# Four-layer graph network on one core: x2 @ w2 computed before layer 2, w3 applied in layer 2, adjacency of layers 2 and 3 from a uint8 copy

## The chip, the cores and the metric

The kernel runs on one core of one Trainium2 chip. The metric is the device time of one launch in microseconds (us). The core's engines are named as in the profile: PE multiplies matrices (PEld is its loading of weights), DVE, ACT and POOL work on rows of SBUF, SP only issues transfers. Each engine works through its own instructions in order and waits on semaphores for the others. A transfer is issued by an engine's queue (SP, ACT or POOL here) and then runs beside the engines.

## The reference, cut to what matters

Input: x of 4096 x 256 floats, adj of 4096 x 4096 floats that are 0 or 1, symmetric, about 32 ones in a row. Every layer is `x = layernorm(x + layer(x))`.

```python
# layer 0
h = concat([x, adj @ x / max(deg, 1)]);  out = relu(h @ W + b)
# layer 1, two steps n = 0, 1;  R = (adj + I) with rows divided by their sums
A  = top_p_attention(Xa)          # per row: softmax of q.k, its largest entries up to a mass of 0.9
Xf = R @ Xf;  Xa = A @ Xa;  Z += Xf @ U1[n].T + Xa @ U2[n].T
out = layernorm(X + Z) * g + b
# layer 2;  edge[i] = sum_j adj[i,j] * adj[j,i]
out = concat([x, adj @ x, edge]) @ weight + bias      # weight: 513 x 256, called w2
# layer 3;  A_norm = (adj + I) scaled by degree^-1/2 on both sides
out = relu((A_norm @ x) @ W + b)                      # W called w3
```

The results of layers 0 to 2 are called x1, x2 and x3 below.

## The kernel before, in words

The 4096 rows are 32 tiles of 128 (`NT`, index `it` of the rows being made, `jt` of the rows being summed over). A product with adj takes for each row tile 32 matmuls of 128x512 into one PSUM bank, one for each `jt`. 512 columns, because the 256 columns of x are held as two halves that add up to x: the upper bits in columns 0 to 255, the rest in 256 to 511. `split` makes them (a DVE mask, an ACT copy, a DVE subtraction), `load_halves` loads a whole matrix in eight chunks of 512 KB through two buffers and splits it into a resident tile `xh`. `transposed` turns a tile of 128x256 with two PE transposes and copies it from PSUM with ACT (buffer `xt`).

*Layer 0* (L215 to L318). POOL loads adj with a cast to uint8 (`a8`, L248), SP stores that copy to `adj8_d` (L249), ACT casts pieces of 128x1024 to the matmul's type (L251), and `adj_matmul` (L168) multiplies. ACT's queue loads x, then w0 and two biases, then w1 and w2t, of which PE makes the query weights `wq_sb` (L227 to L229).

*Layer 1* (two steps, `run_step`). For each row tile it makes the R-product (L652), the row's 4096 logits and exponentials `e`, finds the top-p threshold on DVE, and multiplies by the kept entries: gathered rows (L729), or eight pieces of four transposes of `e` each (L712) with their products (L737). The function `pieces` lays these eight pieces out and lets other work be hung onto them (`ops`, by number of the piece). Rows whose threshold the quick search doesn't reach are put off: their numbers are collected in a list, and one extra tile of such rows in step 0, four in step 1 (`put_off`) are taken up again, from rows gathered by POOL. A put-off tile goes through stages, in which DVE brackets the threshold with probes over the whole row (`bracket`, `settle`); PE sums a flag for it (L554). `advance` runs one stage, `finish` all that are left and then the eight pieces; then come, hung onto the next tile's pieces, `s1` (`mix`: the U products and the residual) and `s2` (two normalizations and the store of x2). Normal tiles are stored by SP, put-off ones scattered by POOL to the rows in their list (`put`, L758) in `x2_d`.

The last two put-off tiles, the third and fourth ("job 2", "job 3"), are finished behind the last normal tile:

```python
for job in jobs:
    last = finish(job, last)
for fs in last:
    for f in fs:
        f()
```

Three row buffers of 16 KB a partition, `es[0..2]`, hold the exponentials in step 1; the two jobs use `es[2]` and `es[0]`.

*Layers 2 and 3* (L1026 on). SP loads x2 back through `load_halves`. POOL loads adj from its float input, 512 KB a piece and four pieces a tile, into the matmul's type (`adj_piece`, L137), four buffers. `l2_end` of a tile stands behind the products of the next tile: it adds the two halves, transposes x2's tile and the sum, multiplies with w2 (four matmuls of 128x256, L1052), adds bias, edge term and residual, normalizes to x3, scales it by dinv (degree^-1/2) and splits it into the halves `yh` for layer 3. `l3_end` scales the summed tile by dinv, adds x3 times dinv squared, transposes, multiplies with w3 (two matmuls, L1075), and ends with relu, residual, normalization and the store.

The order of instructions on each engine is made by a scheduler when the program is built, from the order in which the code issues them and from which buffers are free; the functions below say what is issued, not where it comes to stand.

## Time and profile before

| | us |
|---|---|
| median of 3 runs | 3377.89 (3377.06 to 3378.86) |
| the profiled execution, its own time | 3410.96 |
| its span | 3409.3 |
| PE busy in it | 3032.2 (89%) |
| DVE, ACT, POOL busy | 2382.9 (70%), 1598.1 (47%), 920.8 (27%) |

By stage, from windows on the trace (us of the stage, PE busy, DVE busy, ACT busy, granted PE clock, GB/s moved):

| stage | from, to | length | PE | DVE | ACT | clock | GB/s |
|---|---|---|---|---|---|---|---|
| start | 0, 44 | 44 | 4.4 | 17.2 | 13.2 | 1.00 | 178 |
| layer 0 | 44, 360 | 316 | 316.0 | 270.5 | 170.2 | 1.00 | 136 |
| layer 1, step 0 | 360, 1460 | 1100 | 965.5 | 774.4 | 695.2 | 0.96 | 119 |
| step 1, normal tiles | 1460, 2675 | 1215 | 1106.1 | 1004.6 | 627.5 | 0.96 | 36 |
| last put-off tiles, start of layer 2 | 2675, 2822 | 147 | 64.8 | 95.1 | 25.0 | 0.72 | 80 |
| layer 2 | 2822, 3113 | 291 | 291.0 | 118.3 | 41.1 | 1.00 | 245 |
| layer 3 | 3113, 3409 | 296 | 284.4 | 102.9 | 25.8 | 1.00 | 254 |

The profile is of one execution. Times on its page count from the start of the span. Busy times of engines overlap and don't add up to the span. The stage limits are chosen by eye at the slices in which the picture changes; the layers overlap by a tile or two at them.

### The profile page before, as it was taken

The page shows a single profiled execution, that of the slowest core. Times are in us where ns is not written, and L with a number is a line of the kernel's source. Part 1 is how long each engine was busy: PE and PEld are TensorE (multiplying, and loading weights), DVE is VectorE, ACT ScalarE, POOL GpSimd, SP SyncE. Part 2 cuts the span into 40 slices and gives each one's busy share as a digit, 9 for nine tenths or more (in the row PEclk, how much of TensorE's full clock was granted, in tenths as well). Part 3 has the DMA queues.
Part 4 walks back from the last instruction along what each step waited for, and adds up shares of the span by engine and source line. Part 5 has one row for each costly group of instructions (what it writes and reads, how often), then busy time and mean ns, then how long its engine had stood idle before and what let it go on. Part 6 is the DMA issues. An engine that isn't in the chain of part 4 may idle for free. (4 is left out here: it accounts for less than half of the span.)

```text
span 3409.3 us, 46023 instructions
## 1 busy us (share of the span) xinstructions
PE 3032.2 (89%) x14780; PEld 2486.4 (73%) x14780; DVE 2382.9 (70%) x7082; ACT 1598.1 (47%) x2846; POOL 920.8 (27%) x1170
## 2 busy tenths in 40 slices
PE   5999879999999997789989899989997549999998
PEld 4888667777777775568877677877786437887776
DVE  6888858777777776357988886989799654443333
ACT  4555656666766764455555454645553211111000
POOL 1111246666666664100000001001000112222332
PEclk9999999999999997889999999999999769999999
DMA  8888357777777775141001110011011038888887
GB/s 156 149 141 136 73 98 117 130 135 132 133 131 132 132 133 132 61 131 30 24 22 23 33 38 26 30 32 38 29 38 19 15 103 247 244 247 244 266 270 227
DMA packets 233760, 383.52 MB, mean 112 GB/s; under 512 B 33089, under 2 KB 158849, under 8 KB 233505
## 3 DMA queue, kind: packets, MB, share of 16 engines
q0 software_dynamic: 83328, 238.78, 35.3%
q1 hardware_dynamic: 133200, 125.72, 13.1%
q10 hardware_dynamic: 16976, 15.95, 1.5%
q8 instruction: 120, 1.97, 0.3%
q14 instruction: 136, 1.11, 0.1%
HBM read 423.45 MB, written 57.54 MB: 141 GB/s over the span
## 5 line engine op out<-in xcount | busy, mean ns | idle before, releaser
L652 PE MATMUL acc_r<-xh,adjq 128*128 128x512 f32 x2048 | 615.8, 431 | 31.3 <-ACT adjq L649 21.0
L737 PE MATMUL acc_bank<-xa,at 128*128 128x256 f32 x2304 | 568.2, 388 | 31.0 <-ACT at L715 30.4
L638 POOL DMA_INDIRECT G<-x_d,cols x512 | 498.8, 974 | 331.4 <-PE acc_bank L729 159.7
L737 PEld LDWEIGHTS acc_bank<-xa,at 128*128 128x128 f32 x2304 | 425.5, 194 | 92.7 <-ACT at L715 41.3
L652 PEld LDWEIGHTS acc_r<-xh,adjq 128*128 128x128 f32 x2048 | 379.9, 192 | 131.7 <-ACT adjq L649 46.5
L399 DVE MAX8 cand<-e 128x8 f32<-128x256 f32 x1024 | 381.8, 415 | 130.0 <-ACT e L381 115.8
L649 ACT CAST adjq<-adj 128x512 fp32r<-128x512 uint8 x512 | 316.0, 619 | 312.9 <-issue 94.2
L380 PE MATMUL lg<-kS,q 128*128 128x512 f32 x1104 | 395.6, 444 | 17.8 <-ACT e L381 10.2
L381 ACT COPY e<-lg 128x512 f32<-128x512 f32 x552 | 320.2, 586 | 193.7 <-PE lg L380 171.0
L192 POOL TENSOR_TENSOR rstd<-ve,mhalf 128x1 f32<-128x1 f32 x168 | 103.3, 615 | 899.9 <-DVE ve L190 853.3
L729 PE MATMUL acc_bank<-G,dg 128*128 128x256 f32 x1024 | 275.1, 390 | 33.7 <-DMA G<-x_d,cols 26.7
L496 DVE FIND_INDEX8 cols<-top,e 128x8 uint32<-128x4096 f32 x64 | 282.8, 4419 | 0.0
L168 PE MATMUL acc<-xh,adjt 128*128 128x512 f32 x1024 | 261.5, 407 | 22.7 <-ACT xh L144 18.0
L168 PE MATMUL acc<-yh,adjt 128*128 128x512 f32 x1024 | 257.4, 403 | 3.8 <-DMA adjt<-in_adjt 3.4
L168 PE MATMUL acc<-xh,a 128*128 128x512 f32 x1024 | 258.1, 404 | 1.6 <-ACT a L251 1.6
L729 PEld LDWEIGHTS acc_bank<-G,dg 128*128 128x128 f32 x1024 | 193.9, 193 | 82.7 <-DMA G<-x_d,cols 36.0
L137 POOL DMA_DIRECT2D adjt<-in_adjt x256 | 139.6, 545 | 419.8 <-PE acc L168 316.9
L715 ACT COPY at<-at_ps 128x512 f32<-128x512 f32 x296 | 173.9, 589 | 148.3 <-PE at_ps L712 146.9
L168 PEld LDWEIGHTS acc<-xh,adjt 128*128 128x128 f32 x1024 | 192.3, 191 | 67.9 <-ACT xh L144 19.1
L168 PEld LDWEIGHTS acc<-yh,adjt 128*128 128x128 f32 x1024 | 189.8, 188 | 49.0 <-DMA adjt<-in_adjt 4.1
L168 PEld LDWEIGHTS acc<-xh,a 128*128 128x128 f32 x1024 | 191.4, 189 | 43.9 <-ACT a L251 1.7
L712 PE MATMUL at_ps<-ident,e 128*128 128x128 f32 x1184 | 183.6, 279 | 42.9 <-DVE e L629 29.1
(277 smaller groups left out, 4948.4 us busy)
## 6 DMA issues: line engine op xcount, KB each, us to landing
adjt<-in_adjt POOLq DMA_DIRECT2D x256, 512.0 KB
adj<-adj_d SPq DMA_DIRECT2D x256, 128.0 KB
a<-in_adjt POOLq DMA_DIRECT2D x64, 256.0 KB
adj_d<-a SPq DMA_DIRECT2D x64, 256.0 KB
adjn<-in_adjn POOLq DMA_DIRECT2D x64, 256.0 KB
x_d<-x SPq DMA_DIRECT2D x64, 128.0 KB
G<-x_d,cols POOLq DMA_INDIRECT x512
xf_d<-xf_new SPq DMA_DIRECT2D x64, 128.0 KB
```

Source lines behind the costliest of these rows:

```text
L168: nc.tensor.matmul(acc, a[:, j, :], halves(jt), start=(jt == 0), stop=(jt == NT - 1))
L380: nc.tensor.matmul(pl[:, :LC], q[k], kS[:, s], start=(k == 0), stop=(k == 1))
L381: nc.scalar.copy(l[:, s], pl[:, :LC])
L399: nc.vector.max(dst[:, 8 * g : 8 * g + 8], src[:, g * GW : (g + 1) * GW])
L496: nc.vector.max_index(st["at"][:, 8 * r : 8 * r + 8], t8, st["e"][:, :N])
L638: nc.gpsimd.indirect_dma_start(out=g, out_offset=None, in_=x1_d, in_offset=bass.IndirectOffsetOnAxis(ap=st["at"][:, k : k + 1], axis=0))
L649: nc.scalar.copy(a, cur["a8"][:, g % 2 * GP : (g % 2 + 1) * GP, :])
L652: nc.tensor.matmul(acc_r, a[:, j, :], xf[:, jt, :], start=(jt == 0), stop=False)
L712: nc.tensor.transpose(ps[:, j, :], e[:, (g * G + j) * P : (g * G + j + 1) * P], ident)
L715: nc.scalar.copy(at[:, :G, :], ps[:, :G, :])
L729: nc.tensor.matmul(acc_a, dg[:, k % 4, :], st["G"][k], start=(k == 0), stop=(k == KEPT - 1))
L737: nc.tensor.matmul(acc_a, ats[g][:, j, :], cur["xa"][:, jt, :], start=(jt == 0), stop=(jt == NT - 1))
```

## The change

Four things are changed.

1. Query weights: `w1` and `w2t` are loaded on ACT's queue ahead of x, and no longer behind it and w0.
2. x2 @ w2 before layer 2. A new DRAM matrix `zu_d` of 512 columns takes for each row of x2 its product with the neighbour part of w2 (columns 0 to 255, "z") and with the own part (256 to 511, "u"). `z_room` loads the weights into the row buffer that the two jobs do not use, with four buffers for tiles of x2 and four for results; `zu` transposes a tile, makes two matmuls of 128x512 and copies the result from PSUM with ACT; `zu_tile` loads a tile of x2 and stores the result. The first 16 tiles are hung onto job 2's pieces, the other 16 are issued between job 3's stages, four at each. Rows that were put off are done once more from `h` in `s2` and scattered to `zu_d`. So that every row of `x2_d` that is read has been written, layer 0 stores its x1 of the last tile there too.
3. w3 in layer 2. Layer 2 aggregates z, so that the sum over neighbours needs no w2 product; `l2_end` adds u, loaded from `zu_d`. The new `l2_y`, two tiles later, transposes x3, multiplies with w3, scales by dinv and splits into `yh`; so `l3_end` has no product, and adds the tile's own two halves of `yh` in place of x3 times dinv squared.
4. Adjacency in layers 2 and 3 comes from `adj8_d`, in pieces of 128 KB of uint8 issued by SP (five buffers), cast by ACT to the matmul's type (four buffers).

The diff, cut to the lines that these four points touch:

```diff
...
+    zu_d = dram.tile([N + P, 2 * D], F32, name="zu_d")
...
-    def load_halves(scratch, src, queue):
+    def load_halves(scratch, src, queue, cols=slice(None)):
...
-                queue.dma_start(t, all_rows(src)[:, s, :])
+                queue.dma_start(t, all_rows(src)[:, s, cols])
...
+        w1_sb = l0.tile([DA, D], F32, name="w1_sb")
+        nc.scalar.dma_start(w1_sb, w1)
+        w2t_sb = l0.tile([DA, DA], F32, name="w2t_sb")
+        nc.scalar.dma_start(w2t_sb, w2t)
         x0h = load_halves(l0.tile([P, 4 * J0 * D], F32, name="scratch"), x, nc.scalar)
         w0_sb = load_w(l0, w0, "w0_sb")
         lb_sb = load_bcast(l0, ln_b, "lb_sb")
         b0_sb = load_bcast(l0, b0, "b0_sb")
-        w1_sb = l0.tile([DA, D], F32, name="w1_sb")
-        nc.scalar.dma_start(w1_sb, w1)
-        w2t_sb = l0.tile([DA, DA], F32, name="w2t_sb")
-        nc.scalar.dma_start(w2t_sb, w2t)
...
+            if it == NT - 1:
+                nc.sync.dma_start(rows(x2_d, it), x1[:, it, :])
...
                 ln_apply(h, h, ln_stats(h))
                 put(x2_d, st, h)
+                if "z" in cur and st["tile"] is None:
+                    put(zu_d, st, zu(h))
             return [s1] if n + 1 < STEPS else [s1, s2]
+        def z_room(e):
+            w = e[:, : 4 * D].rearrange("p (c o) -> p c o", c=2)
+            for k in range(2):
+                nc.sync.dma_start(w[:, :, k * D : (k + 1) * D],
+                                  w2[(1 - k) * D : (2 - k) * D, :].rearrange("(c p) o -> p c o", p=P))
+            cur["z"] = {"w": w, "x": e[:, 4 * D : 8 * D].rearrange("p (k o) -> p k o", o=D),
+                        "out": e[:, 8 * D : 16 * D].rearrange("p (k o) -> p k o", o=2 * D), "n": 0}
+        def zu(x):
+            z = cur["z"]
+            xt = transposed(x)
+            ps = ps_acc.tile([P, 512], F32, tag=("acc", "nef")[z["n"] % 2], name="zu_ps", bufs=1)
+            for c in range(2):
+                nc.tensor.matmul(ps, xt[:, c, :], z["w"][:, c, :], start=(c == 0), stop=(c == 1))
+            out = z["out"][:, z["n"] % 4, :]
+            z["n"] += 1
+            nc.scalar.copy(out, ps)
+            return out
+        def zu_tile(i):
+            x = cur["z"]["x"][:, i % 4, :]
+            nc.sync.dma_start(x, rows(x2_d, i))
+            nc.sync.dma_start(rows(zu_d, i), zu(x))
...
-            def finish(job, last):
+            def finish(job, last, todo=(), beside=()):
                 while not advance(job):
-                    pass
+                    for f in todo[:4]:
+                        f()
+                    todo = todo[4:]
+                for f in todo:
+                    f()
                 ops = {}
+                for k, f in enumerate(beside):
+                    ops.setdefault(k * NLC // len(beside), []).append(f)
                 for k, fs in enumerate(last):
-                    ops[k + 1] = fs
+                    ops.setdefault(k + 1, []).extend(fs)
...
-            for job in jobs:
-                last = finish(job, last)
+            todo = []
+            if n > 0:
+                z_room(es[1 - NT % 2])
+                todo = [lambda i=i: zu_tile(i) for i in range(NT)]
+            for k, job in enumerate(jobs):
+                if k + 1 < len(jobs):
+                    last = finish(job, last, beside=todo[: NT // 2])
+                    todo = todo[NT // 2 :]
+                else:
+                    last = finish(job, last, todo)
             for fs in last:
                 for f in fs:
                     f()
@@ -1024,20 +1073,27 @@
     with tc.tile_pool(name="l23", bufs=1, reuse_waits="tile") as l23:
-        w2_sb = load_w(l23, w2[: 2 * D, :], "w2_sb")
+        zh = load_halves(l23.tile([P, 4 * J0 * D], F32, name="scratch"), zu_d[:N, :], nc.sync, slice(0, D))
         w2e_sb = load_bcast(l23, w2[2 * D, :], "w2e_sb")
         b2_sb = load_bcast(l23, b2, "b2_sb")
         w3_sb = load_w(l23, w3, "w3_sb")
         b3_sb = load_bcast(l23, b3, "b3_sb")
-        x2h = load_halves(l23.tile([P, 4 * J0 * D], F32, name="scratch"), x2_d[:N, :], nc.sync)
         yh = [pool.tile([P, NT // 2, 2 * D], F32R, tag="X", name=f"yh{k}") for k, pool in enumerate((xpool, l23))]
-        dinv2 = l23.tile([P, NT], F32, name="dinv2")
-        nc.vector.tensor_mul(dinv2, dinv, dinv)
+        def y_halves(jt):
+            return yh[2 * jt // NT][:, jt % (NT // 2), :]
         def main(it, halves):
             acc = ps_acc.tile([P, 512], F32, tag=("acc", "nef")[it % 2], name="acc")
-            adj_matmul(l23, acc, it, halves, lambda it, c: adj_piece(l23, adjt, it, c, "adjt"))
+            for c in range(NJP):
+                a8 = l23.tile([P, JP, P], U8, tag="a8", name="a8", bufs=5)
+                nc.sync.dma_start(a8, adj8_d[it][:, c * JP : (c + 1) * JP, :])
+                a = l23.tile([P, JP, P], F32R, tag="adjt", name="a", bufs=4)
+                nc.scalar.copy(a, a8)
+                for j in range(JP):
+                    jt = c * JP + j
+                    nc.tensor.matmul(acc, a[:, j, :], halves(jt), start=(jt == 0), stop=(jt == NT - 1))
             return acc
         def l2_end(it, acc):
@@ -1046,48 +1102,59 @@
             nc.vector.tensor_add(nn, nn, acc[:, D:])
             xi = l23.tile([P, D], F32, tag="res", name="x2i", bufs=2)
             nc.sync.dma_start(xi, rows(x2_d, it))
-            xt = transposed(xi, nn)
-            ps = half("mm")
-            for c in range(4):
-                nc.tensor.matmul(ps, xt[:, c, :], w2_sb[:, c, :], start=(c == 0), stop=(c == 3))
+            u = l23.tile([P, D], F32, tag="u", name="u", bufs=2)
+            nc.sync.dma_start(u, rows(zu_d, it)[:, D:])
             nc.vector.tensor_add(xi, xi, b2_sb)
+            nc.vector.tensor_add(u, u, xi)
             t = l23.tile([P, D], F32, tag="t", name="t", bufs=2)
-            nc.vector.scalar_tensor_tensor(t, w2e_sb, nef[:, it : it + 1], ps, op0=ALU.mult, op1=ALU.add)
-            nc.vector.tensor_add(t, t, xi)
-            x3 = l23.tile([P, D], F32, tag="h", name="x3", bufs=2)
+            nc.vector.scalar_tensor_tensor(t, w2e_sb, nef[:, it : it + 1], nn, op0=ALU.mult, op1=ALU.add)
+            nc.vector.tensor_add(t, t, u)
+            x3 = l23.tile([P, D], F32, tag="h", name="x3", bufs=3)
             ln_apply(x3, t, ln_stats(t))
             nc.sync.dma_start(rows(x3_d, it), x3)
+            return x3
+        def l2_y(it, x3):
+            xt = transposed(x3)
+            ps = half("mm")
+            for c in range(2):
+                nc.tensor.matmul(ps, xt[:, c, :], w3_sb[:, c, :], start=(c == 0), stop=(c == 1))
             y = l23.tile([P, 1, D], F32, tag="y", name="y", bufs=2)
-            nc.vector.tensor_scalar(y[:, 0, :], x3, dinv[:, it : it + 1], None, op0=ALU.mult)
+            nc.scalar.activation(y[:, 0, :], ps, AF.Copy, scale=dinv[:, it : it + 1])
             up = l23.tile([P, 1, D], I32, tag="up", name="up", bufs=2)
-            split(up, yh[2 * it // NT][:, it % (NT // 2), None, :], y)
+            split(up, y_halves(it)[:, None, :], y)
         def l3_end(it, acc):
             x3 = l23.tile([P, D], F32, tag="res", name="x3i", bufs=2)
             nc.sync.dma_start(x3, rows(x3_d, it))
             a = l23.tile([P, D], F32, tag="agg", name="agg", bufs=2)
-            nc.scalar.activation(a, acc[:, :D], AF.Copy, scale=dinv[:, it : it + 1])
-            nc.vector.scalar_tensor_tensor(a, acc[:, D:], dinv[:, it : it + 1], a, op0=ALU.mult, op1=ALU.add)
-            nc.vector.scalar_tensor_tensor(a, x3, dinv2[:, it : it + 1], a, op0=ALU.mult, op1=ALU.add)
-            xt = transposed(a)
-            ps = half("mm")
-            for c in range(2):
-                nc.tensor.matmul(ps, xt[:, c, :], w3_sb[:, c, :], start=(c == 0), stop=(c == 1))
-            t = l23.tile([P, D], F32, tag="t", name="t", bufs=2)
-            nc.vector.tensor_add(t, ps, b3_sb)
-            nc.vector.scalar_tensor_tensor(t, t, 0.0, x3, op0=ALU.max, op1=ALU.add)
-            o = l23.tile([P, D], F32, tag="h", name="o", bufs=2)
-            ln_apply(o, t, ln_stats(t))
+            d = dinv[:, it : it + 1]
+            nc.scalar.activation(a, acc[:, :D], AF.Copy, scale=d)
+            own = y_halves(it).bitcast(F32)
+            for part in (own[:, :D], own[:, D:], acc[:, D:]):
+                nc.vector.scalar_tensor_tensor(a, part, d, a, op0=ALU.mult, op1=ALU.add)
+            nc.vector.tensor_add(a, a, b3_sb)
+            nc.vector.scalar_tensor_tensor(a, a, 0.0, x3, op0=ALU.max, op1=ALU.add)
+            o = l23.tile([P, D], F32, tag="h", name="o", bufs=3)
+            ln_apply(o, a, ln_stats(a))
             nc.sync.dma_start(rows(out, it), o)
-        for halves, end in ((lambda jt: x2h[:, jt, :], l2_end), (lambda jt: yh[2 * jt // NT][:, jt % (NT // 2), :], l3_end)):
-            acc = None
-            for it in range(NT):
-                new = main(it, halves)
-                if acc is not None:
-                    end(it - 1, acc)
-                acc = new
-            end(NT - 1, acc)
+        done = []
+        for it in range(NT):
+            acc = main(it, lambda jt: zh[:, jt, :])
+            if it > 1:
+                l2_y(it - 2, done.pop(0))
+            if it > 0:
+                done.append(l2_end(it - 1, last))
+            last = acc
+        l2_y(NT - 2, done.pop(0))
+        l2_y(NT - 1, l2_end(NT - 1, last))
+        for it in range(NT):
+            acc = main(it, y_halves)
+            if it > 0:
+                l3_end(it - 1, last)
+            last = acc
+        l3_end(NT - 1, last)
```

## The prediction

> **What bounds the kernel now.** I read the forty slices first, to find the stages; then the chain of waits; then the timeline where the chain is not the same group over and over; then groups by line in one stage.
>
> ```profile
> PE   5999879999999997789989899989997549999998
> DVE  6888858777777776357988886989799654443333
> ACT  4555656666766764455555454645553211111000
> PEclk9999999999999997889999999999999769999999
> DMA  8888357777777775141001110011011038888887
> ```
>
> PE is at nine tenths in all stages but three: the first slice, the middle (1400 to 1535 us) and the slices around 2640 to 2820 us. The last seven slices are layers 2 and 3: PE full, ACT nearly idle, DMA at eight tenths. Windows on them, clean of their ends:
>
> ```profile
> 2825.00:3113.00 288.00, 288.00 (x1311) 233.55 (x1310) 117.43 (x328) 40.21 (x89) 81.48 (x149) 1.00 0.81 245
> 3134.00:3399.00 265.00, 262.21 (x1141) 206.81 (x1139) 89.87 (x240) 22.35 (x62) 80.68 (x147) 1.00 0.87 264
> ```
>
> So both layers are set by what PE must do, the adjacency DMA hiding behind it (PE waited 3.6 us for it in both together). The chain gives the price of each piece: one tile of layer 2, then one of layer 3.
>
> ```profile
> 2835.10 6.50 PE acc L168 x28
> 2842.04 0.92 PE acc L168 x4
> 2842.96 1.81 PE mm_bank L1052 x8
> ...
> 3170.74 6.75 PE acc L168 x29
> 3177.71 0.86 PE acc L168 x3
> 3178.57 0.88 PE mm_bank L1075 x4
> ```
>
> A layer 2 tile starts every 9.67 us (2835.10, 2844.77), a layer 3 tile every 8.71 (3170.74, 3179.45). 32 acc matmuls take 7.44, the four w2 products 1.80, the two w3 products 0.88, two transposes about 0.22. The tail of layer 1 is another matter: there DVE finds the threshold of the last put-off tile and PE waits.
>
> ```profile
> 2697.74 1.02 POOL L758 DMA_INDIRECT x_d<-h,to_last  x1 [0.74 <-DVE lo_l L468]
> 2734.99 0.19 PE L554 MATMUL mm_bank<-ones_col,bad_l 128*1 128x1 f32 x2 [38.31 <-DVE bad_l L530]
> 2753.75 1.94 PE L712 MATMUL at_ps<-ident,e 128*128 128x128 f32 x8 [18.57 <-DVE e L629]
> 2784.40 1.03 POOL L758 DMA_INDIRECT x_d<-h,to_l  x1 [0.31 <-issue]
> 2789.31 0.93 SPq L158 DMA_DIRECT2D scratch<-x_d  x2
> ```
>
> PE stands idle 38.3 us before the flag matmul and 18.6 us after it: 57 us, the room that the change wants to fill.
>
> **The change part by part.** All sums are against the profiled execution (span 3409.3, its own time 3410.96); the median of the runs is 3377.89, 1% less, so a saving counts 0.99 of itself there.
>
> *Query weights.* PE's first matmul (L227) stands ahead of all others and waits for w2t_sb; ACT's copies of it stand ahead of the first adjacency cast:
>
> ```profile
> 33.28 0.69 PE L227 MATMUL mm_bank<-w2t_sb,w_sb 64*128 64x64 f32 x2 [33.28 <-DMA w2t_sb<-in_w2t]
> 39.92 1.04 ACT L251 CAST a<-a 128x1024 fp32r<-128x1024 uint8 x1
> 41.02 10.31 PE L168 MATMUL acc<-xh,a 128*128 128x512 f32 x37 [1.56 <-ACT a L251]
> ```
>
> In the built program of the change the first cast still stands behind the seventh cast of x, which ends at 38.49 in the trace, but the four wq_sb copies (L229) are out of its way: it can start near 38.9 instead of 39.92. x itself is issued two DMA issues later (0.5 us each). Between a loss of 1.0 and a gain of 1.4 I take a gain of **1.0 us**; layer 0 is PE-bound after it and hands it on. Up to the end of layer 1 the built order is otherwise the same, but for one store of tile 31 to x2_d on SP.
>
> *x2 @ w2 in the tail: the work.* Each of 32 tiles adds, on PE, two transposes (0.22) and two 128x512 fp32 products. No such product exists before; eight 128x256 instructions take 1.73 us on L737 (2769.99, 2772.15 less the transposes), so these are 4 instructions of 0.43, 1.71 us. Together 1.93 a tile, 62 us: more than the 57 us of idle time, even if all of it could be used. ACT adds a copy of 128x256 (0.37, as L180) and one of 128x512 from PSUM (0.59, as L381). SP adds a load of 128 KB and a store of 256 KB.
>
> *Where it stands.* PE runs in order, and the built order puts tiles 0 to 13 among the pieces of the third put-off tile (job 2), then the flag matmul of the last one (job 3), then tiles 14 to 31, and only then job 3's transposes (L712). Followed from 2675, where job 2's pieces begin:
> - Tiles 0 to 5 run between the pieces; job 2's remaining work reaches 2701.8.
> - The load of tile 6 waits on SP for the scatter of tile 31 into x2_d, because that scatter may write any row. The scatter is issued one DVE probe later than now (h is normalized behind the third probe): at 2703.5, not 2697.74. A scatter takes 1.03 to issue and 3.9 more until the next reader starts (2784.40 to 2789.31), and a load about 2: tile 6 at 2710.7. PE is idle for 9 us and starts at half clock (L712 at 2753.75: 1.94 for eight transposes; 1.03 warm), 2 us more.
> - Tiles 6 to 13 with the pieces left take 6.6 us a pair (3.42 products, 0.43 each for transposes, pieces' transposes and one product, 1.3 for three more, 0.6 waiting for ACT's copy): the flag matmul is at about 2737.5 instead of 2734.99. DVE's settling needs it but has slack.
> - Tiles 14 and 15 end at 2741. The other eight pairs have nothing beside them: 3.42 of products, and 1.26 from a pair's end to the next product, since ACT must first copy the old result (0.59), then the transposes (0.37). 4.68 a pair, 37.4 us. PE reaches job 3's transposes near **2778.5; now 2753.75**.
> - Its pieces take 24.6 us to the last product (now 21.9: 1.9 for job 2's rows and 2.4 waiting for their h added, 1.7 saved by a warm PE). So +27 there, and mix and both normalizations as now.
> - Behind h comes the new end: transposes, copy, product (half clock after some 5 us of idleness: 3.4), copy, POOL's scatter behind that of x2_d, landing. From h to the first load of zu it is 10.4 us, against 5.3 from h (2784.0) to 2789.31.
>
> Layer 2's first load thus starts at 2821.5 instead of 2789.31: **+32.2 us**.
>
> *Layer 2's start.* Eight chunks of 512 KB with two buffers. Now it takes 33.2 us to the 64th product (2822.5), beside 512 KB adjacency pieces. After, the pieces are 128 KB, so a round of two chunks is 1.9 of splitting and 4.3 of loading (4.1 at 2789.31 to 2793.42, 4.5 in the first stage). Four rounds and the last nine products: 28.8. **-4.4**.
>
> *Steady layers 2 and 3.* From the 64th product to the last one it is 575.9 us now (2822.5 to 3398.35). Layer 2 loses four w2 products and two transposes but gains two w3 products: exactly a layer 3 tile of now, 8.71. ACT's xt copy now stands behind a cast (1.05) that frees up only when the tile before is through: 0.15 more. 30 tiles: 265.8; the last two tiles' w3 work 2.5; a wait of about 1 for the last x3 at the border. Layer 3 is left with 32 products, 7.48 a tile with the overhead of the rows: 239.4. Sum 508.7: **-67.2**.
>
> The new feed has to carry that. ACT casts four pieces a tile. Layer 0 has the same cast from the same shape:
>
> ```profile
> L168 PE MATMUL acc<-xh,a 128*128 128x512 f32 x783 | 196.9, 403 | 0.0
> L251 ACT CAST a<-a 128x1024 fp32r<-128x1024 uint8 x99 | 103.8, 1049 | 106.0 <-PE acc L168 105.2 <-DMA adj_d<-a 0.8
> ```
>
> PE waits 0.0 us there. Per tile ACT would have 4.2 of casts and 1.6 of other work of 8.86 in layer 2, and 4.7 of 7.48 in layer 3; DVE 3.5 (three at 0.48, two at 0.43, normalization 1.2). POOL loses all adjacency issues; SP takes them (0.32 each, 1.3 us a tile, ahead of and behind its loads and stores: a store waits for DVE, and the casts behind it are up to nine pieces, 17 us, ahead).
>
> *A rule that speaks against it.* In the trace four times as many bytes went through: 245 GB/s in layer 2 with pieces of 512 KB, PE waiting 3.6 us. The Trainium skill ("DMA: Bandwidth & Descriptors", section "Anatomy of one DMA — SWDGE (gpsimd) path") gives a transfer of that path 2.0 us plus its bytes over 436 GB/s: 2.3 us for 128 KB, while PE uses a piece up in 1.86. One at a time, a tile would cost 9.2 us in both layers, 62 of them 570 us, and the 67 would shrink to 6: the change would come out 19 us slower. No run here shows that cost for this piece at this rate; with five buffers five are in flight, so I take the rows. For what stands alone the rule is kinder than the trace: 512 KB would land in 3.2 us (trace 4.1) and the scatter in 2.6 (3.9), some 5 us less at layer 2's start. I keep the trace's.
>
> *The end.* Behind the last product there is no transpose, w3 product or copy: ACT 0.47, three DVE 0.48, two 0.43, normalization 2.3, store 3.5. 8.9 against 10.9: **-2.0**.
>
> Sum: -1.0 + 32.2 - 4.4 - 67.2 - 2.0 = **-42.4**, profiled 3368.5; on the median 0.99 of it, 3377.89 - 42.0 = **3336 us**. Bounds: if the tail hid everything, +6 instead of +32; if none of the 62 us, with its copies 75, were hidden, about +80, which would make it slower.
>
> **The rivals.**
> 1. The tail hides better (scatter and copies sooner, PE warm throughout): +6 to +12. For it: 57 us of idle time. Against: 18 tiles stand behind the flag in the order. 3377.9 - 67 = 3311.
> 2. The feed limits a little: layer 3 stays at 8.1 or layer 2 at 9.3, because ACT's in-order queue holds a cast behind a copy that waits for PE. For it: xt, agg and y stand between the casts. Against: layer 0's 0.0. 20 us less gain: 3356.
> 3. Slower: the transfers of the tail. Each pair loads 256 KB and stores 512 KB; at 4.68 us that is 160 GB/s, beside 247 in layer 2, but in one SP queue in which stores waiting for ACT stand ahead of loads, with four buffers. If a pair takes 7.3 us instead of 4.68 over all 16 pairs, the 42 us are gone; at 9, it is +27: 3405. Against: loads stand four tiles ahead in the built order.
> 4. Nothing to see: tail and steady layers cancel (tail +75), near 3378.
>
> **How the numbers follow.** My sum 0.63, rival 1 0.12, rival 2 0.14, rival 3 0.07, rival 4 0.04. The first three are faster: 0.89; same 0.04; slower 0.07 (0.2%, 7 us, being about what a measurement of this kernel can tell from no change). The range takes in rivals 1 and 2 and the 6 us either way of the pair time: 3306 to 3361; my sum's own range is 3322 to 3350.
>
> **What would show it.** In the changed profile: PE full but for one gap near 2702 to 2711; job 3's L712 transposes some 25 us later; layer 2's chain repeating every 8.7 to 8.9 us without L1052, layer 3's every 7.5 without transposes; DMA share in both far under 0.8 and ACT near 0.6. I am wrong in the tail if layer 2's first load comes before 2805 or after 2835; in the layers if PE waits for casts or a tile takes over 9.2 or 8.0.

## The result, and the profile after

The changed kernel took **3316.99 us** (median of 4 runs, 3311.76 to 3319.24) against 3377.47 of the kernel before; ratio 0.982, 95% interval 0.9803 to 0.9837. Two later comparisons of the same pair, each on another chip, gave 0.9848 (0.9827 to 0.987) and 0.9841 (0.9823 to 0.986). In microseconds the gain was 60 in the first comparison, 48 and 51 in these two. Forecast were 3336 and a range of 3306 to 3361, a gain of 42: faster, as said, and by more than said.

The page of the changed kernel's profile (span 3317.5), its forty slices:

```profile
PE   4999878999999997789989898989999786999998
DVE  5888858878777776357988897888799673444444
ACT  4555566777777774455545454555455333666664
PEclk9999989999999998889999999999999898999999
DMA  8888367777777776241000211011011133333332
```

The three slices of PE's row between 2570 and 2820 us read 7, 8 and 6, where the kernel before had 7, 5 and 4 just ahead of its layer 2: the new products stand there. The layers behind it now show ACT at six tenths, and DMA at three instead of eight. Windows on both layers, clean of their ends (from, to, length, then busy time and instructions of PE, PEld, DVE, ACT and POOL, granted clock, DMA share, GB/s):

```profile
2825.00:3075.00 250.00, 249.62 (x1114) 200.41 (x1114) 107.89 (x321) 162.33 (x238) 16.56 (x30) 1.00 0.35 107
3085.00:3300.00 215.00, 215.00 (x951) 178.01 (x950) 102.73 (x265) 134.27 (x148) 15.88 (x29) 1.00 0.35 106
```

PE is still full in both, the clock is still 1.00, and the traffic is 107 GB/s instead of 245 and 264. The chain of waits gives a tile of layer 2, and the last of layer 3:

```profile
2828.61 0.22 PE tr L180 x2
2828.83 1.39 PE acc L1096 x6
2830.21 0.98 PE mm_bank L1121 x4
2831.19 5.95 PE acc L1096 x26
2837.14 0.22 PE tr L180 x2
...
3289.95 13.84 PE acc L1096 x61
```

From transposes to transposes layer 2 takes 8.53 us (2828.61, 2837.14); layer 3 is one unbroken row of products (61 in 13.84, 0.227 each), and by its normalizations a tile comes every 7.25 us.

PE in the tail, from the timeline (start, length, instruction, idle time before it and who ended it):

```profile
2670.51 1.21 PE L180 MATMUL tr<-ident,e 128*128 128x128 f32 x4 [7.07 <-DMA e<-x_d]
2696.94 0.19 PE L559 MATMUL mm_bank<-ones_col,bad_l 128*1 128x1 f32 x2 [0.45 <-DVE bad_l L535]
2701.71 3.70 PE L844 MATMUL zu_ps<-e,xt 128*128 128x512 f32 x8 [0.51 <-ACT xt L182]
2706.36 3.70 PE L844 MATMUL zu_ps<-e,xt 128*128 128x512 f32 x8 [0.51 <-ACT xt L182]
...
2737.81 1.04 PE L717 MATMUL at_ps<-ident,e 128*128 128x128 f32 x8
```

Two tiles of x2 @ w2 take 4.65 us behind the flag matmul (2701.71, 2706.36). Job 3's transposes (L717) follow with no wait shown. They need only the first quarter of `e` to begin (in a run below they start 0.16 us after it), and DVE had that ready at 2715.66:

```profile
2714.38 1.28 DVE L634 SCALAR_TENSOR_TENSOR e<-e,t_thr_l 128x1024 f32<-128x1024 f32 x1
```

PE comes to them at 2737.81, 22 us later.

### The profile page after: what moved, and what is told of

It reads as the page before. It is cut to its first block, busy times and chain, and to the rows that moved or that the text cites. A ratio compares the mean times of both kernels' runs of the same rounds, so it can differ in the third digit from the quotient of the medians.

```text
span 3317.5 us, 46380 instructions
## 1 busy us (share of the span) xinstructions
PE 3005.6 (91%) x14600; PEld 2455.0 (74%) x14600; DVE 2392.3 (72%) x7113; ACT 1883.1 (57%) x3170; POOL 782.1 (24%) x916
## 5 line engine op out<-in xcount | busy, mean ns | idle before, releaser
L643 POOL DMA_INDIRECT G<-x_d,cols x512 | 499.4, 975 | 300.7 <-PE acc_bank L734 161.9
L1093 ACT CAST a<-a 128x1024 fp32r<-128x1024 uint8 x256 | 268.0, 1048 | 147.5 <-PE acc L1096 119.3
L1096 PE MATMUL acc<-xh,a 128*128 128x512 f32 x1024 | 254.9, 402 | 16.9 <-ACT a L1093 13.2
L170 PE MATMUL acc<-xh,a 128*128 128x512 f32 x1024 | 257.9, 404 | 13.3 <-ACT a L253 13.3
L1096 PEld LDWEIGHTS acc<-xh,a 128*128 128x128 f32 x1024 | 190.5, 189 | 60.3 <-ACT a L1093 15.2
L1096 PE MATMUL acc<-yh,a 128*128 128x512 f32 x1024 | 233.7, 390 | 0.0
L170 PEld LDWEIGHTS acc<-xh,a 128*128 128x128 f32 x1024 | 191.7, 190 | 55.1 <-ACT a L253 13.5
L1096 PEld LDWEIGHTS acc<-yh,a 128*128 128x128 f32 x1024 | 192.1, 188 | 39.8
L253 ACT CAST a<-a 128x1024 fp32r<-128x1024 uint8 x128 | 133.9, 1048 | 129.6 <-PE acc L170 117.4
```

The lines of the kernel that those rows point to most:

```text
L170: nc.tensor.matmul(acc, a[:, j, :], halves(jt), start=(jt == 0), stop=(jt == NT - 1))
L643: nc.gpsimd.indirect_dma_start(out=g, out_offset=None, in_=x1_d, in_offset=bass.IndirectOffsetOnAxis(ap=st["at"][:, k : k + 1], axis=0))
L1093: nc.scalar.copy(a, a8)
L1096: nc.tensor.matmul(acc, a[:, j, :], halves(jt), start=(jt == 0), stop=(jt == NT - 1))
```

## The experiments

**A second profile of the kernel before.** The two profiles differ by 92 us in span, the runs by 60. By the stores of `h` (one a tile), the median tile of step 0 took 28.4 us before and 27.3 after, with the same order of instructions.

> The kernel before, unchanged, for a second profile. In the two profiles so far a tile of step 0 takes 28.3 us before and 27.3 after, 37 us over the stage, though the order of instructions there is the same. Theory: this belongs to the one profiled execution of before (3410.96, its runs 3374 to 3379); here step 0 takes 27.3 to 27.5 us a tile and the span is 3377 +- 4. Rival: the change makes step 0 itself faster (one DRAM matrix more, other addresses); then step 0 stays at 28.3 a tile and the span near 3410.

Measured: span 3368.6, ratio to before 0.9997 (0.9984 to 1.0009), a tile of step 0 every 27.3 us. The slow step 0 belonged to that one execution. From here on this profile is the one to compare with; the two agree in the tail and the layers: 9.68 us a tile in layer 2, 8.71 (median) in layer 3, and the border between tail and layers, the first load of layer 2, stands here in this kernel, and below it in the changed one:

```profile
2749.88 0.94 SPq L158 DMA_DIRECT2D scratch<-x_d  x2
```

```profile
2783.55 0.92 SPq L160 DMA_DIRECT2D scratch<-zu_d  x2
```

**The uint8 adjacency alone.**

```diff
-            adj_matmul(l23, acc, it, halves, lambda it, c: adj_piece(l23, adjt, it, c, "adjt"))
+            for c in range(NJP):
+                a8 = l23.tile([P, JP, P], U8, tag="a8", name="a8", bufs=4)
+                nc.sync.dma_start(a8, adj8_d[it][:, c * JP : (c + 1) * JP, :])
+                a = l23.tile([P, JP, P], F32R, tag="adjt", name="a", bufs=4)
+                nc.scalar.copy(a, a8)
...
```

> The kernel before with one part of the change: adjacency of layers 2 and 3 from the uint8 copy (four buffers of uint8 instead of five, for room). Theory: with less than half of the DMA traffic the products follow each other at 0.228 us, as after, instead of 0.2325 (L3: 7.26 for 32 products), so 0.12 to 0.18 a tile over 62 tiles, 7 to 11 us, and 4.4 at layer 2's start: 11 to 15 us faster, ratio 0.9955 to 0.9967. Rival A: the shorter pitch comes from the layers' having fewer other products between, not from the traffic: 4 us, ratio 0.999. Rival B: ACT, which casts four pieces a tile, holds layer 2 up: not faster.

Measured: ratio 0.9983 (0.9974 to 0.9992), 6 us, nearly what rival A gave. Layer 2 takes 9.72 us a tile, layer 3 8.62, at 82 and 90 GB/s. One tile of its layer 3 in the chain of waits, and below it the row of products in the second profile of the kernel before:

```profile
3200.47 6.03 PE acc L1047 x26
3206.50 0.22 PE tr L178 x2
3206.72 1.40 PE acc L1047 x6
3208.12 0.96 PE mm_bank L1082 x4
```

```profile
3210.56 6.74 PE acc L168 x29
```

The 26 products take 6.03, 0.232 each, the same as before at three times the traffic (29 in 6.74). My theory fell: the traffic is not what stretched the products. Rival A put the shorter pitch of the changed kernel down to there being fewer other products between; the run with w3 put back (below) tests that, and it is not the whole of it.

**The other way round: everything but the uint8 adjacency.** The same edit undone in the changed kernel.

> The changed kernel with adjacency of layers 2 and 3 loaded by POOL as floats, 512 KB a piece, as before. A layer 3 tile then moves 2.1 MB of adjacency and 0.26 MB of x3 and output; the most that a slice of before shows is 270 GB/s. Theory: DMA becomes the bound, 8.7 us a tile in layer 3 (now 7.26) and 9.3 in layer 2 (now 8.53), so 46 and 25 us, and 4 at layer 2's start: near 3385 us, not faster than before; the work taken from PE would be worth nothing without the small adjacency. Rival: 270 GB/s was only what PE asked for; then PE stays the bound, 7.44 and 8.7 a tile: 3317 + 15 = 3332.

Measured: 3429.67 us, ratio 1.0162 (1.0142 to 1.0183): slower than the kernel before, and worse than forecast. What PE waited for in both layers (total, times, longest):

```profile
PE acc L170 <- DMA adjt<-in_adjt: 78.7, 61, 3.1
```

Layer 3 moves 277 GB/s and takes 8.42 us a tile, so 270 was indeed near the most that it gets here. Layer 2 takes 11.1 us at only 223 GB/s, by a ring that I had not seen. From its chain of waits:

```profile
2862.53 0.41 DVE x L199
...
2862.96 0.32 SPq L1107
...
2863.37 6.57 DMA x2i<-x_d
...
2872.85 0.67 POOL rstd L194
```

The load of x2 for the next tile stands on SP behind the store of x3, which waits for DVE, and then takes 6.4 to 6.7 us to land beside 512 KB pieces (2.1 to 3.4 in the changed kernel, beside pieces of 128 KB). DVE waits for it, POOL's part of the normalization (`rstd`) waits for DVE, and the next adjacency loads stand behind that on POOL's queue; the normalized tile is then stored, and the ring begins again. In the changed kernel it does not show: there the chain of layer 2 is PE alone. So the parts are not additive: uint8 alone is worth 6 us, the rest alone costs 56, both together gain 48 to 60.

**Half of the tail's new products left out.** Tiles 16 to 31 are not made, so this kernel leaves part of the computation out.

```diff
+            if it >= NT // 2:
+                nc.sync.dma_start(rows(zu_d, it)[:, :D], x1[:, it, :])
+                nc.sync.dma_start(rows(zu_d, it)[:, D:], x1[:, it, :])
...
-                    last = finish(job, last, todo)
+                    last = finish(job, last)
```

> The changed kernel without the x2 @ w2 products of tiles 16 to 31, those issued between the stages of the last put-off tile (their rows of zu_d hold x1, stored in layer 0). Theory: behind the flag matmul they stand 37 us on PE, of which DVE's settling hides all but 18 (DVE has e ready at 2719.3, PE comes to the transposes at 2737.8 in the changed profile); PE then comes cold, 2 us more: layer 2's first load 16 to 18 us earlier, 3300. Rival A: PE is not what the tail's end waits for, nothing changes: 3317. Rival B: the transfers of these tiles hold more up than PE's time: over 25 us, under 3292.

Measured: 3303.71, span 3298.3; the first load of layer 2 comes 172.2 us after SP's last pair of stores to `x2_d` begins (2591.30 to 2763.49), against 193.9 in the changed kernel. 21.7 of the tail's cost go with these 16 tiles, and PE now waits for DVE's first pass over `e`:

```profile
2716.83 1.94 PE L720 MATMUL at_ps<-ident,e 128*128 128x128 f32 x8 [14.96 <-DVE e L637]
```

```profile
2715.39 1.28 DVE L637 SCALAR_TENSOR_TENSOR e<-e,t_thr_l 128x1024 f32<-128x1024 f32 x1
```

The theory gave 16 to 18, because it took DVE's last pass (2719.3) for what the transposes wait for; by the first pass PE was 22 us late, and that is what came back. In the times it is less: the ratio to before is 0.9797 (0.9779 to 0.9816) where the changed kernel has 0.982 to 0.985, some 8 to 17 us.

**The changed kernel again, with the query weights and w3 put back, each by itself.**

> The changed kernel, unchanged, beside the next three on one chip: ratio 0.982 as before. In its profile as in the first: first load of layer 2 some 194 us behind the last store of a normal tile to x2_d, layer 2 at 8.53 and layer 3 at 7.25 us a tile, 13.7 us from the last product to the end. Rival: those were that one execution's own; then they move by some us here.

Measured: 193.2 us to the first load, 8.51 and 7.25 a tile, 13.7 at the end. The readings hold.

```diff
         b0_sb = load_bcast(l0, b0, "b0_sb")
+        w1_sb = l0.tile([DA, D], F32, name="w1_sb")
+        nc.scalar.dma_start(w1_sb, w1)
...
```

> The changed kernel with w1 and w2t loaded behind x and w0 again. In the profiles the store of step 0's first tile starts at 491.1 to 493.4 with the weights behind x and at 495.9 to 496.5 with them ahead. Theory: the two loads ahead of x cost 2 us until the first product (43.02 against 41.02) and some 2 more in layer 0: this store comes back to 491 to 493, 3 to 5 us faster than the changed kernel, ratio to it 0.9987. Rival, the prediction's own step: being ahead gains 1 us; then 1 us slower.

Measured: the first store of `h` comes at 493.6 instead of 497.5, span 3318.8 against 3322.0. In the times it is lost: ratio to before 0.9845 against 0.9848, each with an interval of 0.0043. The profile says a loss of 3 to 4 us from loading the weights first, which the runs can neither show nor refute.

```diff
-            nc.scalar.activation(y[:, 0, :], ps, AF.Copy, scale=dinv[:, it : it + 1])
+            nc.vector.tensor_scalar(y[:, 0, :], x3, dinv[:, it : it + 1], None, op0=ALU.mult)
...
+            xt = transposed(a)
+            ps = half("mm")
+            for c in range(2):
+                nc.tensor.matmul(ps, xt[:, c, :], w3_sb[:, c, :], start=(c == 0), stop=(c == 1))
```

> The changed kernel with w3 applied in layer 3 again (y = dinv * x3 is split in layer 2; transposes, product and bias in layer 3). Theory: PE has the same products to do; layer 2 runs at 7.25 to 7.35 us a tile and layer 3 at 8.5 to 8.6, the sum 15.8 as now, and the end is 1 to 2 us longer: the changed kernel + 1 to 3 us. So the whole saving in the layers comes from w2. Rival A: layer 2 cannot go under 8 us, because each tile also loads u and x2 and stores x3 on SP's queue between the adjacency pieces: + 20 us. Rival B: two products that break up the row of adjacency products cost more where both layers' ends are, + 10.

Measured: 3325.6 against 3320.74, ratio to before 0.9863 (0.9844 to 0.9882) beside 0.9848: not told apart by the times. Layer 2 takes 7.55, layer 3 8.50 a tile, 16.05 together against 15.76. Moving w3 is worth 0.3 us a tile at most, 9 us; the rest of the layers' 83 comes from moving w2 out of them, together with the uint8 adjacency without which it does not pay. Layer 2, now without transposes and products, is the fast one, and layer 3 with them the slow one. That layer 2 stays 0.3 above 7.25 has a place: its first ten tiles or so run at 7.25, and from then on one product a tile, the first of a piece, starts up to 0.7 us late. ACT's copy of `yh` waits there for DVE's split, with two casts behind it in ACT's queue:

```profile
2995.79 0.41 ACT L146 CAST yh<-up 128x256 fp32r<-128x256 f32 x1 [2.94 <-DVE up L145]
```

Layer 3 of this run also answers the question left by the uint8 run, since it has the same breaks in its rows of adjacency products (two transposes, w3 products) as that run's layer 3:

```profile
3200.68 5.91 PE acc L1096 x26
3206.60 0.22 PE tr L180 x2
3206.82 1.39 PE acc L1096 x6
3208.21 0.97 PE mm_bank L1135 x4
```

Here the 26 products take 5.91, 0.227 each; there they took 0.232. The 32 products of a tile take 7.30 here, 7.43 there and 7.25 unbroken. So the breaks account for about 0.05 a tile, and neither they nor the traffic for the other 0.13. What makes the products slower in the kernel before and in its uint8 version stays open.

**Where the new products stand: three tries.** First the room for them goes into the tile of the R-product's matrix, which is free from tile 30 on, and 12 tiles are hung onto tile 30's pieces.

```diff
+                if n > 0 and i == NT - 2:
+                    z_room(hpool.tile([P, 16 * D], F32, tag="H", name="zroom"))
+                    later_zu = [lambda i=i: zu_tile(i) for i in range(NT)]
+                    for k, f in enumerate(later_zu[:12]):
+                        at(k * NLC // 12, f)
...
-                    last = finish(job, last, beside=todo[: NT // 2])
+                    last = finish(job, last, beside=todo[:14])
```

> The changed kernel with the room for x2 @ w2 in the tile that held the matrix of the R-product (free once the last R-product is made), so that 12 of the 32 tiles go beside the pieces of normal tile 30, 14 beside job 2's pieces, and 6 between job 3's stages. Theory: PE is idle for 24 us from tile 30's pieces to tile 31's, where the 12 fit; behind the flag matmul only some 5 tiles are left, which DVE's settling hides; layer 2's first load comes 15 to 20 us earlier: near 3300, ratio to before 0.977. Rival A: the 12 tiles hold tile 30's and 31's own chain up by what they take on PE (23 us): nothing gained, 3317. Rival B: their copies on ACT and their loads on SP's queue delay the settling too: slower than the changed kernel.

Measured: 3318.3 against 3320.74, not told apart by the times, where 3300 was forecast. In the profiled execution the first load of layer 2 comes 10.7 us earlier than in the changed kernel beside it (2777.51 against 2788.22). Job 3's transposes now wait for DVE, but job 2's start 8 us later (2625.76 against 2617.61). They come 8.11 us after PE's last work ahead of them, here and in the two kernels below alike (13.65 of idle time in the changed kernel); the loop over left-over rows (L903) stands between, and the 12 tiles ahead of it pushed it back. That entering the loop costs these 8 us is argued from the place of the gap and not shown. Rival A, for the most part.

Then other places, and beside them the changed kernel once more:

> The changed kernel, unchanged, on the same chip as the next three, so that they can be compared with it: ratio to before 0.982 to 0.985. No theory differs on it.

Measured: 3315.73, ratio 0.9841.

```diff
+        def zu_load(i):
+            nc.sync.dma_start(cur["z"]["x"][:, i % 16, :], rows(x2_d, i))
...
+                for i in range(6, 22):
+                    zu_load(i)
             for k, job in enumerate(jobs):
...
-                    last = finish(job, last, beside=todo[: NT // 2])
+                    last = finish(job, last, beside=todo[:20])
```

> The changed kernel with the room for x2 @ w2 in the tile of the R-product's matrix, which is free from tile 30 on: 6 tiles beside normal tile 30's pieces (the twelve of the last experiment took 13 us too long there), 20 beside job 2's pieces, 6 between job 3's stages; 16 buffers for tiles of x2 instead of 4, and tiles 6 to 21 loaded ahead of the scatter of tile 31, on which the seventh load waits now for 7 us. Theory: the bound of the tail is then DVE's settling of the last put-off tile, no longer PE's row of products: the transposes of job 3 come right after DVE's e, layer 2's first load 16 to 20 us earlier than in the changed kernel; 3301 to 3305, ratio to it 0.9945. Rival A: the flag matmul, now behind 20 tiles, holds the settling up: 8 us less gain. Rival B: the six tiles beside tile 30 delay tile 31 by what they take, 12 us: then only some 6 us are left.

Measured: 3305.16 against 3315.73, ratio to before 0.9811 (0.979 to 0.9831); the span is 3303.6 against 3321.1, the first load of layer 2 at 2767.68 against 2785.47, 17.8 earlier. The load's wait of 7 us is gone, and DVE ends both of PE's waits in the tail:

```profile
2703.03 0.19 PE L559 MATMUL mm_bank<-ones_col,bad_l 128*1 128x1 f32 x2 [2.77 <-DVE bad_l L535]
2721.85 1.06 PE L717 MATMUL at_ps<-ident,e 128*128 128x128 f32 x8 [1.05 <-DVE e L634]
```

The bound has gone over from PE to DVE's settling, and the load came as early as the theory said. The times gained less than the spans, 10.6 us (ratio 0.9968 to the changed kernel, forecast 0.9945); the profiled execution of the changed kernel was the slowest of its four. What is left of the tail's cost, about 14 us (32.0 less 17.8), stands outside this stretch: some 10 of it behind the start of job 3's transposes, from where the first load is 45.8 us off here, 44.3 to 45.7 in the three profiles of the changed kernel, and 35.6 in the kernel before.

```diff
-        zh = load_halves(l23.tile([P, 4 * J0 * D], F32, name="scratch"), zu_d[:N, :], nc.sync, slice(0, D))
+        zh = load_halves(l23.tile([P, 4 * J0 * D], F32, name="scratch"), zu_d[:N, :], nc.sync, slice(0, D), 2)
```

> As the one before, with the query weights behind x again (2 to 4 us) and layer 2's matrix loaded in 16 chunks of 256 KB through four buffers instead of 8 of 512 KB through two. Theory: splitting and loading then overlap better, 64 products are through 25 us after the first load instead of 28.6: 6 to 8 us below the one before. Rival: half of the bytes a transfer cost what the overlap gains; then 2 to 4 us below, from the weights alone.

Measured: **3302.27 us**, ratio to before 0.9799 (0.9777 to 0.982), span 3299.1, 4.5 below the one before, where 6 to 8 were forecast: the first 96 products of layer 2 end 35.5 us after the first load instead of 39.1, as the theory had it for 64, and the first store of `h` comes at 494.9 instead of 497.9. Of these 3 us only 0.6 are left at the first load of layer 2 (2767.05 against 2767.68). It is the lowest time of all kernels with the whole computation, 13 us under the changed kernel's 3315.73 on the same chip; against the one before, the times alone do not separate it.

**The end.**

```diff
-                nc.sync.dma_start(a8, adj8_d[it][:, c * JP : (c + 1) * JP, :])
+                nc.gpsimd.dma_start(a8, adj8_d[it][:, c * JP : (c + 1) * JP, :])
```

> The changed kernel with the uint8 pieces of layers 2 and 3 issued by POOL instead of SP. In all kernels with the uint8 adjacency the last store is followed by 8.6 us until the span's end, in those with float adjacency by 3.5; SP's last wait is for PE's sequencer, 6 us against 0.7 to 1.0. Theory A: it hangs on the pieces being issued by SP; then 3.5 here. Theory B: it hangs on PE's taking its weights from ACT's casts (its waits on semaphores); then 8.6 here too. Layer 2 and 3 per tile as before, 8.53 and 7.25, by both.

Measured, one run: 3313.56, layers 8.5 and 7.25. SP's last waits, in the changed kernel and then here:

```profile
SPq L1195 <- PEq L1195: 6.6, 2, 6.0
SPq L1195 <- DMA out<-o: 1.0, 1, 1.0
```

```profile
SPq L1195 <- PEq L1195: 1.5, 2, 1.0
SPq L1195 <- DMA out<-o: 1.0, 1, 1.0
```

From the last output of DVE to the end it is 3.6 us instead of 8.7. Theory A: the wait for PE's sequencer hangs on who issues the pieces. The other runs agree: 5.7 us with uint8 alone, issued by SP, and 1.0 with float pieces issued by POOL. Why PE's sequencer comes 5 us later when SP issues them stays open.

## Why the prediction was right, point by point

The clean pair of profiles (spans 3368.6 and 3317.5, from separate comparisons) can be cut at the prediction's own joints. The first is the start of the last pair of stores that SP makes to `x2_d`, at 2587.95 and 2589.66; the 64th product of layer 2 is at 2783.07 and at 2812.3 (the 16th of the 48 from 2808.52 to 2819.91); the last product ends at 3357.96 and 3303.79.

| step | predicted | measured |
|---|---|---|
| start, up to that store | -1.0 | +1.7 |
| tail, to the first load of layer 2 | +32.2 | +32.0 (161.9 to 193.9) |
| layer 2's start, 64 products | -4.4 | -4.4 (33.2 to 28.8) |
| steady layers 2 and 3 | -67.2 | -83.4 (574.9 to 491.5) |
| the end | -2.0 | +3.1 (10.6 to 13.7) |
| sum | -42.4 | -51.0 |

The first comparison's 60 us are 9 more than this pair shows. No step of the table has them, and the two later comparisons, with 48 and 51, do not either.

*The tail* was right in its mechanism, in its price of a pair (4.68 forecast, 4.65 measured), and nearly in the idle gap at a load behind the scatter (9 forecast, 7.07 measured). That its sum came out within 0.2 us is in part luck: two errors cancelled. The second profile of the kernel before has job 3's transposes here:

```profile
2714.30 1.94 PE L712 MATMUL at_ps<-ident,e 128*128 128x128 f32 x8 [18.72 <-DVE e L629]
```

Counted from the pair of stores, that is 126.35 us, and 148.15 in the changed kernel: PE came to them 21.8 late, where the prediction had 24.8. From there to the first load it was 45.7 instead of 35.6, 10.2 more, where the prediction had 7.4; job 3's pieces, with job 2's rows among them, took 5 us longer instead of the 2.7 forecast. The step that made the first part too large: the gap did not make the flag matmul late. Job 2's pieces with the new products between them ran from 2637 to 2697, and PE still had to wait 0.45 us for DVE there. The lateness arose behind the flag, and leaving the 16 late tiles out gave it back (21.7); the other 10 stayed.

*The steady layers* were the term that was mis-sized, by 16 us, in both halves. I carried the pace of the products over from the kernel before: 32 of them at 7.44. In the changed kernel they take 7.25 in layer 3, which gives 7 us (7.48 forecast with the overhead of the rows). In layer 2 I put 8.71, a layer 3 tile of before, and 0.15 for ACT's copy behind a cast; it came out at 8.53, 10 us over 30 tiles. ACT's delay did not show: PE waited 0.4 us in all in layer 2's window. With uint8 alone the same tile takes 8.62, not 8.71; the remaining 0.09 are nearly all in the pace of the products (26 in 5.95 instead of 6.03). That the products would run faster was no part of the reasoning, and its cause is not found: the traffic is excluded, and the breaks between them explain only some of it.

*The end* lost 3.1 us where I had 2.0 of gain: the arithmetic behind the last product is shorter, 5.0 from the last product to the last normalization's output, but from there to the end it is 8.7, where I had put 3.5 for the store: SP's closing wait grew by 5. *The start* cost some 4 us by the store of `h`, where I gave it 1 of gain. I had priced the two loads ahead of x by their issue alone, 0.5 us each; x's first piece landed 11 us later, as DVE's first step on it shows, before (second profile) and after:

```profile
4.97 0.69 DVE L143 TENSOR_SCALAR scratch<-scratch 128x1024 int32<-128x1024 int32 x1 [3.88 <-DMA scratch<-in_x]
```

```profile
16.03 0.69 DVE L145 TENSOR_SCALAR scratch<-scratch 128x1024 int32<-128x1024 int32 x1 [14.95 <-DMA scratch<-in_x]
```

The first product comes at 43.02 instead of 41.02. Only 1.7 of the 4 us show in the table: from the first store of `h` to the pair of stores it takes between 2091 and 2098 us in the ten profiles that share this stretch.

*The rule weighed against the change*, 2.3 us for 128 KB alone (the Trainium skill, "DMA: Bandwidth & Descriptors", section "Anatomy of one DMA — SWDGE (gpsimd) path"), would, as an estimate, have made the tile 9.2 us. That figure is for transfers issued by POOL, and these pieces are issued by SP, but the issues on the page of the changed kernel (KB each, median us to landing) show that a single piece takes as long here:

```profile
a<-adj_d SPq DMA_DIRECT2D x256, 128.0 KB, 2.3
```

But tiles of 8.53 and 7.25 show that the pieces overlapped, so the price of one alone was never paid.

*The rivals.* The feed by ACT (rival 2) did not limit. The tail's transfers (rival 3) did not either: the pairs ran at 4.65 (their 768 KB make 168 GB/s at 4.68, not the 160 of the prediction). Rival 1, a tail that hides more, was not what this kernel did; moved to other places the products came nearer to it, from +32.0 to about +14.

*The scale.* I scaled by 0.99 since the profiled execution was 1% above its median. The second profile shows that its surplus of 41 us lay almost all in step 0 (37 between its first and last stores of `h`), not in the stages that the change touches: nothing there wanted scaling. It hardly moved the sum here (0.4 us).

## What to carry to other kernels

A pace read from the kernel before need not hold in the kernel after: the same products took 0.232 us there and 0.227 here, and 0.2 to 0.3 us a tile were 16 us over two layers. A load put ahead of others costs them more than its issue: two small ones delayed x's first piece by 11 us. Two parts of a change can be worth little or less than nothing alone and much together (6 and -56 us here, 48 to 60 together): taking work from PE pays only when the transfers behind it shrink too, and shrinking them pays only when PE has less to do. Where work is moved into an engine's idle time, ask what stands behind it in that engine's queue: the same 32 products cost 32 us or about 14 by which wait they were put in front of, and with 12 of them in a good-looking hole the times showed no gain. An agreement of a sum says little on its parts: the tail's came out right with two of its parts off by some 3 us, one up and one down.

## What the runs showed of the hardware that was not expected

- With adjacency pieces issued by SP, the closing wait of SP for PE's sequencer is 6.0 us; with POOL issuing the same pieces 1.0.
- A third of the DMA traffic (82 to 90 GB/s in place of 245 to 264) left the pace of 128x512 products where it was, 0.232 us each. In the changed kernel they take 0.227 at 106 GB/s with nothing between them, and with w3 put back also 0.227 with the same transposes and products between them as at 0.232. The cause is open.
- A load of x2 of 128 KB beside 512 KB pieces took 6.4 to 6.7 us to land (2.1 to 3.4 beside 128 KB pieces), and through one in-order queue it set the pace of a whole layer at 223 GB/s, well under the 277 of the next one.
